# A gated-slot-attention kernel with a Strassen-like product: E's transposes ahead of the 64 by 64 products, and sums, silu pieces and weight pieces in other places

## The chip, the core and the metric

The kernel runs on one core of a Trainium2 chip. The core has TensorE (PE, whose weight loads are shown apart as PEld), VectorE (DVE), ScalarE (ACT), GpSimd (POOL) and SyncE (SP), which here issues all DMAs. The time is device microseconds of one execution. Smaller is better. A profile of one execution gives start and length of every instruction and what released an engine that waited.

## The reference, cut to what matters

Two layers on x of 2 batches by 2048 tokens by 512, all in float32: gated slot attention with 16 heads, and a feed-forward part with a Hadamard transform. Each is added to its input and followed by a layer norm.

```python
q, k, v, s = (to_heads(x @ W) for W in (Wq, Wk, Wv, Ws))     # 64, 64, 128, 64 wide a head
s = clip(s, -32, 32); z = cumlogsumexp(s, time)
g = exp(z[t-1] - z[t]); p = exp(s - z)
hk[t] = hk[t-1] * g + outer(k, p);   ok = q * 64**-0.5 @ hk   # slots of the keys
pv = softmax(ok)
hv[t] = hv[t-1] * g + outer(p, v);   o = pv @ hv
o = o * rsqrt(mean(o**2) + 1e-5) * g_norm_weight
x = layernorm(x + (o * silu(x @ Wg)) @ Wo)
h = fwht(silu(x @ W1.T) * (x @ W3.T))                        # 2048 wide
x = layernorm(x + h @ W2.T)
```

## The kernel before

**Products.** Every large product is done as two by two blocks with seven products in place of eight. Each product needs sums of blocks of both factors, which are made ahead, and its results are added up in PSUM and SBUF afterwards. `LEFT` and `RIGHT` say which of a factor's seven slices product m takes. The order of the seven differs from place to place. For a weight, `Weights` loads three of its blocks into slices 0 to 2 and the fourth into a tile `low`, of which there is one for all weights, and `sums(0)` to `sums(3)` make slices 3, 5, 4 and 6: sum 0 and sum 1 read `low`, sum 2 reads sum 0, sum 3 reads sum 2. Slice 6 is taken by product 3, slice 3 by 5, slice 4 by 6, slice 5 by 7.

**Attention.** The 16 heads go in four groups of four, and each group walks over 16 chunks of 128 tokens, both batches at once: 64 steps. `run(new, now, before, old)` writes out one round by hand and works on four steps at a time: `new` gets its x, `now` makes q, k, s (the products `main("q", k)`, L521) and v, g (`main("v", k)`, L547) and its own slots, `before` makes its values and begins its output product `o` (L764, with `o(1)`, `o(5)`, `o(2)`), and `old` finishes it (`o(3)`, `o(6)`, `o(7)`, `o(4)`; the sums of o into the rows are L760). The order on PE, DVE, ACT and POOL is the order of the text; only SP's queue is ordered by a scheduler. Between the q and the v products stands a block of small products:

- `exp_s`: DVE clips s (L529), ACT takes the exponential twice (e2 in L533, e in L535; a group's first step takes one), POOL adds what was carried (L534).
- `k_transposed` (L567, ACT copies to kr in L569), then `o(4)`.
- `scores` (L598), `scores2` (L673), `share_of_keys` (L608), `share_of_values` (L685): 64 by 64 arrays of PE, sixteen products each. DVE masks the scores (L602, L679) and takes in the shares (L620). The scores lie in PSUM banks 2 and 3, the shares of the values in banks 0 and 1.
- `e_transposed`: four 128 by 128 transposes of e into bank 3 (L573), copied by ACT to eT (L575), which `scores2` reads one step later. Then `running_sum` (L580), whose sums ACT copies (L582) and DVE inverts (`reciprocal`, L591).
- `slots` (L626), `values` (L696), `state_slots` (L635), `state_values` (L705): 64 by 64 arrays again.

After the block come the v products 6, 5, 2, 7, 3, 4; `gated` (ACT L722, DVE L724 and L726, POOL L728 to L731) and `softmax` (DVE L643 to L651, ACT L652, DVE L656 and L657, POOL L658, DVE L662) lie beside them. `o_transposed` (L748) is copied by ACT (L445, L446), DVE and POOL (L448 to L451) into ob, and `silu` (L561) gates.

**A group's end.** In a group's last step (`last`) the next q, k, s weights are loaded and summed, and the next v, g weights loaded, to be summed in the first step of the next group (`changes`). One step later (`o_last`) the next Wo rows are loaded, scaled by half the norm's weight (L438) and summed. All of these sums are DVE's, but Wo's scaling and its second and fourth sum, which are POOL's.

**Weight pieces.** The sums of W1, W2 and W3 for the feed-forward part, and in the last group those of the new x (`block`), are generators that do one piece at each call. A round calls them at places 2, 3 and 4 (`work_on`) and at its end; the last four chunks also call them in `more`.

**Feed-forward.** For each of 8 blocks of x and 4 sets of hidden rows (a unit u), `up` makes seven products of seven (L235). DVE adds the results up (L216), twice a sum of two accumulators is taken (L250, for products 6 and 7), `silu` gates the four results (ACT L193) and leaves the products with the other half and the sums for `down` to POOL, in two pieces each two and three slots later. The first unit begins in the last two rounds of attention and runs beside `last_block`, which prepares the last block's x (transposes L315, DVE differences L321).

Of the kernel before, what the change touches and what calls it, by code (L numbers as in the profile page):

```python
# [9 lines left out]
F32 = mybir.dt.float32  # L10
# [5 lines left out]
P = 128  # L16
# [4 lines left out]
DV = 128  # L21
# [17 lines left out]
def gated_slot_attention_ffn_kernel(  # L39
# [34 lines left out]
    nc.gpsimd.memset(mhalf, -0.5)  # L74
    gn = const.tile([P, 1], F32, name="gn")
    nc.sync.dma_start(out=gn, in_=gnw.rearrange("(p o) -> p o", o=1))

    within = const.tile([P, TH], F32, name="within")
    for h in HALVES:
# [102 lines left out]
    def silu(h, at, src):  # L182

        if at == 11:
            h["hid"] = fp.tile([P, 2, 7, 2 * TQ], F32, name="hid")
            h["a21"] = fp.tile([P, 2, 2 * TQ], F32, name="a21", bufs=1)
        a21 = h["a21"]
        hid = h["hid"]
        place = {11: hid[:, :, 0], 21: hid[:, :, 1], 22: hid[:, :, 2], 12: a21}[at]
        o = place.rearrange("p i (j t) -> p i j t", j=2)  # L190
        v = src.rearrange("p (i j) t -> p i j t", j=2)
        gate, lin = v[:, :, :, 0:TQ], v[:, :, :, TQ:]
        nc.scalar.activation(o, gate, AF.Silu)  # L193

        def piece(i):
            nc.gpsimd.tensor_tensor(o[:, i], o[:, i], lin[:, i], ALU.mult)  # L196
            if at == 12:
                nc.gpsimd.tensor_tensor(hid[:, i, 5], hid[:, i, 0], a21[:, i], ALU.subtract)  # L198
            elif at == 22:
                nc.gpsimd.tensor_tensor(hid[:, i, 3], a21[:, i], hid[:, i, 2], ALU.add)  # L200
                nc.gpsimd.tensor_tensor(hid[:, i, 4], hid[:, i, 3], hid[:, i, 0], ALU.subtract)
            elif at == 21:
                nc.gpsimd.tensor_tensor(hid[:, i, 6], hid[:, i, 1], hid[:, i, 4], ALU.subtract)

        for i in range(2):
            after(2 + i, lambda i=i: piece(i))

    def up(u, h):

# [8 lines left out]
        for i, m in enumerate(OUTER):  # L218
            w, left, right = wt.pop(0), LEFT, xb[RIGHT[m]]
            if i < 6 or u + 1 < NU:  # L220
                wt.append(load_w(u + (i + 1) // 7, (i + 1) % 7))
            to, first = {5: ("v", None), 3: ("w", "v"), 1: ("u", None), 2: ("x", "u")}.get(m, ("u", "u"))
            if to == "v" and "v" not in acc:
                open_acc("v", tag="h2")
            if to == "w" and "w" not in acc:
                open_acc("w", pool=fp)
            if i == 3:
                h["w2"] = w2p.tile([P, 2, 7, HD], F32, name="w2t")
                for j in range(2):
                    nc.sync.dma_start(out=h["w2"][:, j], in_=w2s[p + j * NSET])  # L230
            c = sums(pch, 2 * TQ, "")
            for k in INNER:
                s = c[SUM[k]]
                for j in range(2):
                    nc.tensor.matmul(  # L235
                        s[:, j * TQ : (j + 1) * TQ], lhsT=w[:, LEFT[k], j, :], rhs=right[:, RIGHT[k], :],
                        start=(k in (1, 2, 5) and j == 0), stop=True, skip_group_check=True,
                    )
                b = BLOCK[k]
                if k in (1, 5, 6, 4):  # L240
                    if first is None:
                        nc.scalar.copy(t[to][:, b], s)
                    else:
                        add(t[to], s, b, t[first])
                else:
                    add(t[to], s, b)
                if m in (6, 7) and k in ENDS:
                    o = t["w" if m == 6 else "v"][:, b]

                    (nc.gpsimd if u else nc.vector).tensor_tensor(o, o, t["u"][:, b], ALU.add)  # L250
                if k == 4:
                    if p == NSET - 1 and blk + 1 < NBLK:
                        load_x(blk + 1, RIGHT[m])
                    if m in (2, 6, 7, 4):
                        at, src = {2: (11, "x"), 6: (12, "w"), 7: (22, "v"), 4: (21, "u")}[m]
                        silu(h, at, t[src])
                yield
# [36 lines left out]
    def last_block():  # L294
# [17 lines left out]
        for i, (b, k) in enumerate(todo):  # L312
# [5 lines left out]
            if b:  # L318
                for dst, a, c in ((t1, b12, b11), (b12, b22, b12), (t2, b22, t1), (t4, b21, t2)):
                    dst, a, c = (e[:, :, at] for e in (dst, a, c))  # L320
                    nc.vector.tensor_tensor(dst, a, c, ALU.subtract)  # L321
            yield
        yield
        for m, src in enumerate(parts):
# [25 lines left out]
    with ExitStack() as att:  # L350
# [40 lines left out]
        class Weights:  # L391


            def __init__(self, name, parts, raw=None, pool=wp):
                width = sum(p[1] for p in parts)
                self.t = pool.tile([P, 7, 2, width], F32, name=name)
                self.low = c1.tile([P, 2, width], F32, name="low", tag="low")
                self.raw = raw
                at = 0
                for src, n in parts:  # L400
                    for (i, j), dst in (
# [5 lines left out]
                        )  # L407
                    at += n

            def sums(self, k):  # L410
                t, low = self.t, self.low

                second = nc.vector if self.raw is None else nc.gpsimd
                if k == 0:
                    if self.raw is not None:
                        self.raw(t[:, 0:3])
                        self.raw(low)
                    nc.vector.tensor_tensor(t[:, 3], low, t[:, 2], ALU.add)
                elif k == 1:
                    second.tensor_tensor(t[:, 5], t[:, 0], low, ALU.subtract)  # L420
                elif k == 2:
                    nc.vector.tensor_tensor(t[:, 4], t[:, 3], t[:, 0], ALU.subtract)
                else:
                    second.tensor_tensor(t[:, 6], t[:, 1], t[:, 4], ALU.subtract)

        def rows_of(src, g, width):
            return lambda j: src[j * HD : (j + 1) * HD, g * width : (g + 1) * width]
# [5 lines left out]
            return Weights("wvg", [(rows_of(a, g, HG * DV), HD) for a in (wv, wg)])  # L433

        def load_o(g):
            def scaled(a):

                nc.gpsimd.tensor_scalar(a, a, gn, 0.5, ALU.mult, ALU.mult)  # L438

            at = g * HG * DV  # L440
            return Weights("wo_", [(lambda j: wo[at + 2 * j * DV : at + (2 * j + 2) * DV, :], HD)], scaled, wpo)

        def right_factor(dst, tp):

# [36 lines left out]
        class Step:  # L481
# [88 lines left out]

            def e_transposed(self):
                for i in range(NQ):
                    nc.tensor.transpose(bank(3)[:, i, :], self.e[:, i, :], ident)  # L573
                self.eT = c2.tile([P, NQ, P], F32, name="eT")
                nc.scalar.copy(self.eT, bank(3))  # L575

            def running_sum(self):
                p = pch.tile([P, 512], F32, name="running", tag="c1", bufs=2).rearrange("p (i t) -> p i t", t=P)
# [454 lines left out]
        def run(new, now, before, old):  # L1033
# [12 lines left out]
                        next(ups)  # L1046

            def work_on(place):
                y["place"] = place
                next(pieces[0], None)  # L1050

            def more():

                if old is not None and old.g == NG - 1 and old.n >= NCB - 4:
                    work_on(1)


            g = now.g if now is not None else NG
            last = now is not None and now.final and g + 1 < NG
            o_last = old is not None and old.final and old.g + 1 < NG  # L1060
            opens = now is not None and now.first
            o_opens = o_last or now is steps[0]

            changes = opens and now is not steps[0]

            late = [nw["vg"].sums] if now is steps[0] else []
            if opens:
                w["qks"] = nw.pop("qks")
            main("q", 1)
            do(old, "o", 3)  # L1070
            if new is not steps[1]:
                do(new, "load_x")
            main("q", 2)
# [1 line left out]
            y["second"] = new is not None and new.g > 0  # L1075
            work_on(2)
            if changes:
                nw["vg"].sums(0)
            main("q", 5)
            work_on(3)  # L1080
            if changes:
                nw["vg"].sums(1)
            main("q", 6)
            do(old, "o", 6)
            do(before, "r_transposed")
            if changes:
                nw["vg"].sums(2)
            main("q", 7)
            work_on(4)
            if changes:  # L1090
                nw["vg"].sums(3)
            main("q", 3)
            main("q", 4)
            do(old, "o", 7)
# [16 lines left out]
            do(old, "row_stats", 0)  # L1111
            if o_last:
                nw["o"] = load_o(old.g + 1)

# [3 lines left out]
            do(before, "within2")  # L1120
            do(now, "share_of_keys")
            do(before, "share_of_values")
            do(now, "e_transposed")
            do(now, "running_sum")
            do(old, "normalize")
            do(old, "store_rows")
# [11 lines left out]
            for f in late:  # L1138
                f(1)
            main("v", 5)  # L1140
            do(now, "reciprocal", 1)
            main("v", 2)
            more()
            for f in late:
                f(3)
            if last:
                nw["qks"].sums(0)
            main("v", 7)
            do(now, "softmax")
            main("v", 3)  # L1150
            more()
            if o_opens:
                nw["o"].sums(0)
            do(now, "softmax_sum")
            if o_opens:
                nw["o"].sums(1)
            do(before, "o_transposed")
            if o_opens:
                nw["o"].sums(2)
                nw["o"].sums(3)  # L1160
            do(now, "softmax_end")
            main("v", 4)
            if last:
                nw["vg"] = load_vg(g + 1)
                nw["qks"].sums(1)
            do(now, "tanh")
            if before is not None and before.first:
                w["o"] = nw.pop("o")
            do(before, "o", 1)
            if last:  # L1170
                nw["qks"].sums(2)
            do(before, "o", 5)
            more()
            do(now, "silu")
            do(before, "o", 2)
            if last:
                nw["qks"].sums(3)
            next(pieces[0], None)

            if old is not None and old.g == NG - 1 and NCB - 4 <= old.n < NCB - 2:  # L1180
                rows_transposed_last(old)
# [109 lines left out]
```

## Time and profile before

| | |
|---|---|
| median of 3 executions | 3583.42 us (3582.95 to 3586.16) |
| the profiled execution | 3586.86 us |
| its span, first to last instruction | 3584.7 us |
| mean granted PE clock | 0.996 |
| DMA, mean share of 16 engines | 35.2% |
| a plain step of attention | 36.9 to 38.0 us |
| first product of the first unit beside the rounds | about 2470 us |

The profile is read from the page's shares by engine, then by the waits (who waited for whom, with total, count and longest), then in order of time. A line of that last view has start, length, engine, line, operation, output <- input, form and count of merged instructions, and in brackets how long the engine was idle before and what released it. In order of time the instructions of one step's small products are seen to start 1026.67 (L567), 1028.07 (L598), 1029.51 (L685), 1030.64 (L573), 1031.13 (L580), 1032.09 (L626), 1035.03 (L547).

### The profile page before, as it was taken

What the parts mean: (1) busy time and instruction counts of PE and PEld (TensorE: products, weight loads), DVE (VectorE), ACT (ScalarE), POOL (GpSimd) and SP (SyncE); (2) the same over time, 40 slices, a digit from 0 to 9 for tenths busy, and PEclk for the clock granted to TensorE, in tenths of its full rate; (3) what the DMA queues carried; (4) which work ended last, traced back from release to release, by engine and by line L of the source; (5) the groups of instructions that cost most, each with busy time, mean ns of one, the idle gap of its engine ahead of it and who ended that gap; (6) DMA issues with size and microseconds to landing.
All of it is one profiled execution on the core that took longest, in us unless ns stands there. A gap on an engine that the chain in (4) does not pass through costs nothing. (4 is left out here: it accounts for less than half of the span.)

```text
span 3584.7 us, 76033 instructions
## 1 busy us (share of the span) xinstructions
PE 3505.6 (98%) x32160; PEld 2749.4 (77%) x32160; DVE 2379.1 (66%) x3968; ACT 985.3 (27%) x1768; POOL 1108.0 (31%) x1048
## 2 busy tenths in 40 slices
PE   8999999999999999999999999998899999999998
PEld 6777777777777767777767777766788888888887
DVE  5677677756567756567666677777666766756756
ACT  3333333233333233333333333332111111111110
POOL 2222222212112222212213222223353553553544
PEclk9999999999999999999999999999999999999999
DMA  4433434421112321112221233346636535435432
GB/s 156 123 108 111 140 113 130 128 67 53 63 60 67 116 72 54 65 60 67 83 88 61 66 116 119 131 139 232 210 131 237 182 126 208 161 130 198 167 128 75
DMA packets 229188, 425.08 MB, mean 119 GB/s; under 512 B 20592, under 2 KB 141808, under 8 KB 228848
## 3 DMA queue, kind: packets, MB, share of 16 engines
q1 hardware_dynamic: 228848, 420.22, 35.2%
q8 instruction: 253, 4.15, 0.5%
q14 instruction: 87, 0.71, 0.1%
HBM read 297.47 MB, written 125.30 MB: 118 GB/s over the span
## 5 line engine op out<-in xcount | busy, mean ns | idle before, releaser
L547 PE MATMUL c<-wvg,xb 128*128 128x512 f32 x1792 | 808.0, 596 | 4.5 <-DVE t L479 2.3
L547 PEld LDWEIGHTS c<-wvg,xb 128*128 128x128 f32 x1792 | 321.8, 189 | 365.9 <-issue 289.1
L521 PE MATMUL c<-xb,wqks 128*128 128x128 f32 x3584 | 559.3, 279 | 6.7 <-DVE rows L760 5.0
L521 PEld LDWEIGHTS c<-xb,wqks 128*128 128x128 f32 x3584 | 485.2, 194 | 35.2 <-DVE rows L760 20.0
L216 DVE TENSOR_TENSOR accux<-c,accux 128x512 f32<-128x512 f32 x496 | 340.9, 690 | 180.0 <-PE c L235 163.7
L274 PE MATMUL dc<-w2t,hid 128*128 128x256 f32 x1792 | 455.3, 379 | 2.1 <-DVE res L281 2.1
L235 PE MATMUL c<-wvg,xb 128*128 128x256 f32 x1792 | 431.9, 380 | 7.1 <-DVE accux L216 7.1
L760 DVE TENSOR_TENSOR rows<-c,rows 128x256 f32<-128x256 f32 x448 | 182.1, 417 | 349.6 <-PE c L764 348.0
L235 PEld LDWEIGHTS c<-wvg,xb 128*128 128x128 f32 x1792 | 338.7, 190 | 57.8 <-DVE accux L216 11.2
L274 PEld LDWEIGHTS dc<-w2t,hid 128*128 128x128 f32 x1792 | 340.2, 190 | 49.5 <-DVE res L281 3.3
L521 PE MATMUL c<-wqks,xb 128*128 128x128 f32 x1792 | 350.5, 278 | 2.0 <-DMA wqks<-in_L_attn_Ws 2.0
L479 DVE TENSOR_TENSOR t<-c,kept 128x384 f32<-128x384 f32 (+1 forms) x384 | 229.8, 610 | 168.9 <-PE c L521 164.0
L235 PE MATMUL c<-wqks,xb 128*128 128x256 f32 x1344 | 326.5, 381 | 8.4 <-DVE accv L216 3.0
L474 ACT COPY kept<-c 128x384 f32<-128x384 f32 (+1 forms) x384 | 203.1, 529 | 418.5 <-PE c L521 335.6
L235 PEld LDWEIGHTS c<-wqks,xb 128*128 128x128 f32 x1344 | 255.0, 191 | 47.5 <-DVE accux L216 5.0
L521 PEld LDWEIGHTS c<-wqks,xb 128*128 128x128 f32 x1792 | 275.8, 194 | 2.3 <-DMA wqks<-in_L_attn_Ws 2.3
L281 DVE TENSOR_TENSOR res<-dc,res 128x256 f32<-128x256 f32 x448 | 189.0, 422 | 117.6 <-PE dc L274 106.9
L591 DVE RECIPROCAL iz<-z 128x256 f32<-128x256 f32 x128 | 223.8, 1748 | 45.7 <-ACT z L582 45.7
L728 POOL TENSOR_SCALAR ss<-ss 128x8 f32<-128x8 f32 x64 | 12.6, 197 | 770.7 <-DVE ss L726 770.7
L534 POOL TENSOR_TENSOR e<-e,zc 1x512 f32<-1x512 f32 x60 | 76.4, 1274 | 541.1 <-ACT e L533 539.4
L724 DVE TENSOR_TENSOR t<-po,t 64x512 f32<-64x512 f32 (+1 forms) x192 | 132.3, 689 | 120.3 <-ACT sq L722 119.4
L250 POOL TENSOR_TENSOR accw<-accw,accux 128x512 f32<-128x512 f32 x60 | 75.9, 1275 | 283.1 <-DVE accux L216 281.7
(194 smaller groups left out, 5084.8 us busy)
## 6 DMA issues: line engine op xcount, KB each, us to landing
xb<-w13s SPq DMA_DIRECT2D x112, 896.0 KB
xb<-xd SPq DMA_DIRECT2D x48, 896.0 KB
yd<-rows SPq DMA_DIRECT2D x128, 256.0 KB
w2t<-w2s SPq DMA_DIRECT2D x32, 896.0 KB
rows<-yd SPq DMA_DIRECT2D x100, 256.0 KB
xd<-xb SPq DMA_DIRECT2D x16, 896.0 KB
wvg<-fxd SPq DMA_DIRECT2D x16, 896.0 KB
raw<-in_L_ffn_W SPq DMA_DIRECT2D x48, 256.0 KB
```

The lines of the kernel that those rows point to most:

```text
L216: nc.vector.tensor_tensor(into[:, b], s, (into if first is None else first)[:, b], ALU.add)
L235: nc.tensor.matmul(s[:, j * TQ : (j + 1) * TQ], lhsT=w[:, LEFT[k], j, :], rhs=right[:, RIGHT[k], :], start=(k in (1, 2, 5) and j == 0), st ...
L274: nc.tensor.matmul(s, lhsT=h["hid"][:, i, LEFT[m], k * P : (k + 1) * P], rhs=h["w2"][:, i, RIGHT[m], :], start=(m in (1, 2, 5) and i == 0) ...
L281: nc.vector.tensor_tensor(r, s, r, ALU.add)
L474: nc.scalar.copy(self.kept[k], s)
L479: nc.vector.tensor_tensor(t[:, to], s, self.kept[other], ALU.add)
L521: nc.tensor.matmul(out[:, i * P : (i + 1) * P], lhsT=a, rhs=b, start=(k in OPENS and c == 0 and i == 0), stop=(c == 1), skip_group_check=True,
L534: nc.gpsimd.tensor_tensor(self.e2[0:1], self.e2[0:1], zc, ALU.add)
L547: nc.tensor.matmul(out, lhsT=self.xb[:, RIGHT[k], c, :], rhs=w["vg"].t[:, LEFT[k], c, :], start=(k in OPENS and c == 0), stop=(c == 1), sk ...
L591: nc.vector.reciprocal(self.iz[:, h], self.z[:, h])
L724: nc.vector.tensor_tensor(self.gj[to, j], self.po[j][at], self.gj[to, j], ALU.mult)
L760: nc.vector.tensor_tensor(y_, self.uo.sum(k), y_, ALU.add)
```

## The change

- `e_transposed` stands behind `o(4)`, ahead of the scores, and writes bank 1 instead of bank 3.
- The next group's q, k, s sums: 0, 1 and 3 on POOL, 2 on DVE, the first two ahead of v's product 7, the others behind `o(5)`. The v, g sums: 1 and 3 on POOL.
- Wo's scaling is ACT's (`scale_o`), behind v's product 5; its sums 0, 1 and 3 are POOL's, the first two ahead of v's product 7, the others ahead of `o_transposed`. In the first step all of it stands at the round's end, the sums on DVE.
- Weight pieces are called at places 1 to 4, where 1 stands behind `o(3)`, and not at a round's end. In a group's first round they aren't called.
- In the first unit the sum for product 6 is POOL's, and `last_block`'s differences are. In every unit the first silu's pieces run five slots later.

```diff
+    half_gn = const.tile([P, 1], F32, name="half_gn")
+    nc.gpsimd.tensor_scalar(half_gn, gn, 0.5, 0.0, ALU.mult, ALU.add)
...
-            after(2 + i, lambda i=i: piece(i))
+            after(2 + i + (5 if at == 11 else 0), lambda i=i: piece(i))
...
-                    (nc.gpsimd if u else nc.vector).tensor_tensor(o, o, t["u"][:, b], ALU.add)
+                    (nc.gpsimd if u or m == 6 else nc.vector).tensor_tensor(o, o, t["u"][:, b], ALU.add)
...
-                    nc.vector.tensor_tensor(dst, a, c, ALU.subtract)
+                    nc.gpsimd.tensor_tensor(dst, a, c, ALU.subtract)
...
-            def sums(self, k):
+            def sums(self, k, eng=nc.vector):
...
-                    nc.tensor.transpose(bank(3)[:, i, :], self.e[:, i, :], ident)
+                    nc.tensor.transpose(bank(1)[:, i, :], self.e[:, i, :], ident)
...
-                nc.scalar.copy(self.eT, bank(3))
+                nc.scalar.copy(self.eT, bank(1))
...
             def work_on(place):
-                y["place"] = place
-                next(pieces[0], None)
+                if not changes:
+                    y["place"] = place
+                    next(pieces[0], None)
+
+            def scale_o():
+                for t in (nw["o"].t[:, 0:3], nw["o"].low):
+                    nc.scalar.activation(t, t, AF.Copy, scale=half_gn)
...
             do(old, "o", 3)
+            work_on(1)
...
             if changes:
-                nw["vg"].sums(1)
+                nw["vg"].sums(1, nc.gpsimd)
...
             if changes:
-                nw["vg"].sums(3)
+                nw["vg"].sums(3, nc.gpsimd)
...
             if o_last:
                 nw["o"] = load_o(old.g + 1)
+            do(now, "e_transposed")
...
             do(before, "share_of_values")
-            do(now, "e_transposed")
             do(now, "running_sum")
...
             main("v", 5)
+            if o_last:
+                scale_o()
             do(now, "reciprocal", 1)
             main("v", 2)
...
             if last:
-                nw["qks"].sums(0)
+                nw["qks"].sums(0, nc.gpsimd)
+                nw["qks"].sums(1, nc.gpsimd)
+            if o_last:
+                nw["o"].sums(0, nc.gpsimd)
+                nw["o"].sums(1, nc.gpsimd)
             main("v", 7)
             do(now, "softmax")
             main("v", 3)
             more()
-            if o_opens:
-                nw["o"].sums(0)
             do(now, "softmax_sum")
-            if o_opens:
-                nw["o"].sums(1)
+            if o_last:
+                nw["o"].sums(2)
+                nw["o"].sums(3, nc.gpsimd)
             do(before, "o_transposed")
-            if o_opens:
-                nw["o"].sums(2)
-                nw["o"].sums(3)
             do(now, "softmax_end")
             main("v", 4)
             if last:
                 nw["vg"] = load_vg(g + 1)
-                nw["qks"].sums(1)
             do(now, "tanh")
...
             do(before, "o", 1)
+            do(before, "o", 5)
+            more()
             if last:
                 nw["qks"].sums(2)
-            do(before, "o", 5)
-            more()
+                nw["qks"].sums(3, nc.gpsimd)
             do(now, "silu")
             do(before, "o", 2)
-            if last:
-                nw["qks"].sums(3)
-            next(pieces[0], None)
+            if now is steps[0]:
+                scale_o()
+                for k in range(4):
+                    nw["o"].sums(k)
```

More of the change, by code (lines that the diff above doesn't have):

```diff
@@ L391, in gated_slot_attention_ffn_kernel, with __init__ @@
         class Weights:
-            def __init__(self, name, parts, raw=None, pool=wp):
+            def __init__(self, name, parts, pool=wp):
                 width = sum(p[1] for p in parts)
@@ L397, in __init__ @@
                 self.low = c1.tile([P, 2, width], F32, name="low", tag="low")
-                self.raw = raw
                 at = 0
@@ L408, in __init__ @@
                     at += n
-            def sums(self, k):
+            def sums(self, k, eng=nc.vector):
                 t, low = self.t, self.low
-                second = nc.vector if self.raw is None else nc.gpsimd
                 if k == 0:
[L415 to L418, printed above, removed]
+                    eng.tensor_tensor(t[:, 3], low, t[:, 2], ALU.add)
                 elif k == 1:
-                    second.tensor_tensor(t[:, 5], t[:, 0], low, ALU.subtract)
+                    eng.tensor_tensor(t[:, 5], t[:, 0], low, ALU.subtract)
                 elif k == 2:
-                    nc.vector.tensor_tensor(t[:, 4], t[:, 3], t[:, 0], ALU.subtract)
+                    eng.tensor_tensor(t[:, 4], t[:, 3], t[:, 0], ALU.subtract)
                 else:
-                    second.tensor_tensor(t[:, 6], t[:, 1], t[:, 4], ALU.subtract)
+                    eng.tensor_tensor(t[:, 6], t[:, 1], t[:, 4], ALU.subtract)
         def rows_of(src, g, width):
@@ L435, in load_o @@
         def load_o(g):
-            def scaled(a):
-                nc.gpsimd.tensor_scalar(a, a, gn, 0.5, ALU.mult, ALU.mult)
             at = g * HG * DV
-            return Weights("wo_", [(lambda j: wo[at + 2 * j * DV : at + (2 * j + 2) * DV, :], HD)], scaled, wpo)
+            return Weights("wo_", [(lambda j: wo[at + 2 * j * DV : at + (2 * j + 2) * DV, :], HD)], wpo)
         def right_factor(dst, tp):
@@ L1055, in more @@
                     work_on(1)
+            changes = now is not None and now.first and now is not steps[0]
             g = now.g if now is not None else NG
@@ L1061, in run @@
             opens = now is not None and now.first
-            o_opens = o_last or now is steps[0]
-            changes = opens and now is not steps[0]
             late = [nw["vg"].sums] if now is steps[0] else []
@@ L1077, in run @@
             if changes:
-                nw["vg"].sums(0)
+                nw["vg"].sums(0, nc.vector)
             main("q", 5)
@@ L1086, in run @@
             if changes:
-                nw["vg"].sums(2)
+                nw["vg"].sums(2, nc.vector)
             main("q", 7)
```

## The prediction

> **What bounds the kernel now.** I read the page's busy shares, then the busy time of the stretches between one step's first scores and the next, then TensorE's (PE's) waits, then the instructions in order of time where those point.
>
> ```profile
> PE 3505.6 (98%) x32160; PEld 2749.4 (77%) x32160; DVE 2379.1 (66%) x3968; ACT 985.3 (27%) x1768; POOL 1108.0 (31%) x1048
> ```
>
> PE is the bound and the number of its products stays, so only its pauses can be won. The stretches (us, then busy time of PE, weight loads, VectorE (DVE), ScalarE (ACT), GpSimd (POOL), granted clock, DMA):
>
> ```profile
> 599.40:643.12 43.72, 38.79 (x429) 28.35 (x429) 35.39 (x54) 12.77 (x24) 6.75 (x6) 1.00 0.56 172
> 679.96:724.66 44.70, 40.24 (x406) 30.12 (x405) 30.05 (x48) 12.61 (x25) 14.83 (x11) 0.92 0.35 107
> 1139.51:1176.37 36.86, 36.79 (x421) 27.30 (x421) 26.57 (x39) 12.15 (x24) 8.02 (x7) 1.00 0.17 55
> 1213.40:1255.95 42.55, 37.92 (x422) 27.48 (x421) 33.67 (x50) 11.76 (x23) 10.94 (x14) 1.00 0.48 151
> 1294.07:1339.90 45.83, 40.22 (x412) 29.84 (x411) 24.50 (x36) 13.78 (x27) 14.65 (x11) 0.96 0.24 76
> 1825.72:1868.36 42.64, 39.02 (x422) 28.96 (x421) 31.40 (x42) 11.76 (x23) 6.75 (x6) 0.96 0.38 122
> 1905.01:1947.86 42.85, 38.71 (x406) 28.73 (x405) 25.36 (x38) 11.68 (x23) 14.65 (x13) 0.96 0.19 60
> ```
>
> Row three is a plain step. Against it, and less 0.9 and 1.3 us for weight pieces' products in rows one and five, the steps in which a head group ends (rows 1, 4, 6) lose 6.0, 5.7 and 5.8 us, those that take in the new Wo (2, 5, 7) 7.8, 7.7 and 6.0: 39 us. Of it 8.8 is half clock: (1 - clock) by length gives 3.6, 1.8, 1.7, 1.7. The other place is the feed-forward part's first unit, 2505 to 2550.
>
> ```profile
> PE c L764 <- POOL wo__6775 L424: 3.6, 1, 3.6
> PEld ps L573 <- DVE a L679: 18.8, 62, 1.2
> ...
> 1026.67 0.63 ACT L535 ACTIVATE e<-e 128x512 f32<-128x512 f32 x1
> 1027.11 1.03 PE L764 MATMUL c<-wo__6775,ob 128*128 128x256 f32 x4
> 1030.63 0.42 PEld L573 LDWEIGHTS ps<-ident,e 128*128 128x128 f32 x4 [0.31 <-DVE a L679]
> 1035.03 0.30 PEld L547 LDWEIGHTS c<-wvg,xb 128*128 128x128 f32 x2 [0.17 <-issue]
> ...
> 2021.91 1.03 PE L764 MATMUL c<-wo__17915,ob 128*128 128x256 f32 x4
> 2022.40 0.63 ACT L535 ACTIVATE e<-e 128x512 f32<-128x512 f32 x1
> ...
> 696.00 1.54 POOL L438 TENSOR_SCALAR wo__6775<-wo__6775,gn 128x1536 f32<-128x1536 f32 x1
> 696.66 1.42 DVE L651 TENSOR_TENSOR r<-r,mx 128x512 f32<-128x512 f32 x1
> ...
> 2429.43 0.71 PE L521 MATMUL c<-xb,wqks 128*128 128x128 f32 x4 [1.86 <-DVE rows L760]
> 2509.34 2.67 POOL L196 TENSOR_TENSOR hid<-hid,accux 128x512 f32<-128x512 f32 x2
> 2509.40 2.88 DVE L95 TENSOR_SCALAR rows<-rows,mv,lrs 128x512 f32<-128x512 f32 x2 [0.95 <-POOL lrs L91]
> ```
>
> The reader is to see three things. A return from 64 by 64 arrays to the full one idles the weight loads 0.17 us without a wait, 0.31 with L679's. The exponentials e (L535) are ready at 1027.30, 0.7 before PE could start behind L764 (four starts 0.22 apart: 1027.97); in the last group at 2023.03, 0.25 after 2022.78. And a DVE operation from SBUF to SBUF beside one of POOL waits for it: L651 takes 0.69 alone, here it ends 0.54 after L438 ends, and two L95 (0.54 each) end behind L196. Results that DVE reads from PSUM (L760, L216) aren't lengthened beside POOL.
>
> **A, E's transposes.** Start to start a plain step has 0.31 from L764 to the scores, 0.34 from L685 to L573, 0.49 to L580, 0.96 to L626: 2.10. After: 0.22 to L573, 0.33, 0.20 to the scores (as behind L567 at 58.15), 0.20 from L685 to L580 (as from L705 to L547), 0.32 + 0.43 + 0.31: 2.01. So -0.09 in 48 steps, -4.5: the wait's 0.14 goes, but L580 restarts slower than a transpose. Behind it: `share_of_values` waits for eT's copy (bank 1), done about 0.8 before; L602, L679, L620 end 0.43 later, the last at 1032.46, when L591 can't start before 1032.7. In 13 steps of the last group PE waits for e, 0.25 and 0.11 for signal and restart, less the 0.18 wait for kr that this hides: +2.4. Step 63 sheds 0.8 of a 1.15 wait for L679. Sum -2.9 (from -8, no wait or restart left, to +3).
>
> **B, the group's sums.** L658, a POOL sum of 128x512, takes 1.28; by length a q/k/s sum (768) 1.9, a v/g sum (1024) 2.6. On DVE they take 0.94 and 1.22.
> - Group's end, 17.5 in three. DVE's sum before v7 (L418, 2.08) goes to POOL, which is free from 614.98. L651, ready at 615.7, must let it end at 616.9: +1.05 (0 to 1.9). After o5 DVE keeps one sum of 0.94 ahead of L561 and o2's L760, which q2 awaits: +1.35 (0.95 to 3.1, where POOL's last sum gets in before L561; L651's row says that the earlier runs first, and L561 is, so 1.35). The waits of 1.8 and 1.2 us for o3 and q5 go, since sums and weight pieces no longer stand there. On SP's queue all v/g pieces now stand behind `low`, which waits for POOL's sum until 619.3 (issued at 623.96 in the profile); 2 MB at some 300 GB/s land by 628. The first v/g sum waits for them on DVE, o6's L760 and q7's L479 behind it, q4 behind those: +0.5 (0 to 1.6). Left 2.9 each: -8.8.
> - New Wo, 21.5 in three. The scaling (POOL 1.54 and 1.12) becomes two ACT operations of 1.5 and 0.6 (from `th`, 1.06 for 1024), on an ACT idle from 691.6 to 698.1; its DMAs were issued by 681.7, and L652 stands behind: 0 (to +1). Two sums on POOL stand before L658; L651 waits +0.4. DVE's sum stands before L448: o5 +0.7 (0.3 to 1.2). POOL's last stands before L450, and L662 lets it pass: o3 and q2 +1.2 (0.4 to 3). L424's wait and the half clock go. Left 2.3 each, and 2.0 at 1299.7 that no engine caused: -12.6.
> - The first group's sums come later, as many: 0 (-1 to +1.5). `half_gn`, one POOL instruction of 0.2 while POOL has nothing until 8.2: 0.
>
> Sum -21.4.
>
> **C, weight pieces.** The call at a step's end moves behind the next o3; none run in a group's first step. At 2427 four DVE pieces stand before o3's L760: the 1.86 and the half clock behind it (2430 to 2434, 1.7) go: -3.6. In 14 steps a piece's product fills the 0.23 that PE waits before q2: -3.2 (to 0). Else DVE is idle where they land (1.65 before L760 at 1025.15). Sum -6.8.
>
> **D, first unit.** L196 five slots later frees L95: 1.9 of the 2.96 us that PE waits at 2510. Four L250 (0.69) and eight L321 (0.42) leave DVE; PE waits 0.7, 1.7 and 1.1 beside them. POOL needs 3 us for each four L321, then 5.1 for L250, and the next sums wait for that: 1.0 back. Sum -4.4 (-8 to 0).
>
> The profiled execution took 3586.86 (span 3584.7), 3.4 above the median of 3583.42; differences against its span are applied to the median: 3583.4 - 35.5 = 3548.
>
> **Rules against the rows.** The three waits over 3 us in rows two, five and seven each have half clock behind them, those of 1.8, 0.5 and 1.2 in a row one time in three; I leave none over 1.4 and take none. The Trainium skill, page TensorE: Matmul & The Clock Gate, section "Part 1: The HAM clock gate", gives one idle window of about 3.4 us as the trigger; by it the last group's end would not have halved, and the row shows it did, so a remainder stays possible (rival 1). Its page GPSIMD Engine Reference, section "3.1 Elementwise", measures a `tensor_tensor` add at 1.96 times VectorE's time and says to keep such work on VectorE. An estimate by that, 5 us longer in each of three groups if POOL were what is waited for, would make the sum 3563. The rows have POOL busy 8 of 37 us, and I follow them.
>
> **Rivals.**
> 1. POOL's sums hold DVE up and the clock still halves: 0.85 + 1.75 more in three group ends (7.8), 1.7 in four steps (6.8), D nothing (4.4): 3567. For it L651's row; against it POOL's idle time before its sums.
> 2. DVE slips in between: lower ends of B (-5.9 and -4.8) and D (-3.6): 3534. For it: PSUM reads don't wait.
> 3. It cancels: A at +3, a quarter of B, C and D nothing: 3581. Against it: L424's wait alone is 3.6 and surely goes.
> 4. Slower: weight pieces between q7 and `exp_s` make e late in every step, at L573 before the scores. To pass 3590.6 it must outweigh the other parts' 32.6 by 7.2, 0.83 in each of 48 steps, so e 1.5 us later than now. At 1.7 it gives 3599. Before L529 DVE has 0.71 and 1.65 idle, and the longest piece is two sums of 1.0.
>
> **Numbers.** Forecast 0.57 (own range 3538 to 3558), rivals 0.20, 0.10, 0.06, 0.07. The range 3533 to 3571 leaves out rivals 3 and 4 and some of 1 and 2. The measurement tells 0.2% (7.2 us): faster 0.87, same 0.06, slower 0.07.
>
> **What would show it.** L573 behind L764 without L679's wait, and waiting for e in the last group only; the six late steps at 39 to 40 us with the clock mostly at 1.00; POOL sums of 1.9 with L651 over 1 us; no L521 wait at 2427; no L250 `accw` on DVE. I am wrong if q2's waits at a group's end exceed 2 us, or if L535 releases PE in plain steps.

## The result, and the profile after

The changed kernel takes 3613.72 us (median of 4 runs, 3608.76 to 3617.14) beside 3584.79 us of the kernel before (4 runs, 3582.95 to 3587.48). The ratio is 1.0078, 95% interval 1.0064 to 1.0092: slower by 28 us (23 to 33). The forecast was 3548 us, faster. The profiled execution of the changed kernel took 3608.76 us (span 3607.0), 22 us over that of before.

Lines of the changed kernel stand some six lower from L430 on (E's transposes were L573 and are L567, kr's copy L569 and L563, the sums of o L760 and L754, q's sums L479 and L473) and three or four higher before that (L196 is L199, L95 is L98, L235 is L239). The page's busy shares:

```profile
PE 3513.8 (97%) x32160; PEld 2747.3 (76%) x32160; DVE 2354.6 (65%) x3940; ACT 994.7 (28%) x1776; POOL 1142.8 (32%) x1069
```

PE has as many products, so the time is in its pauses again. The stretches from step to step (us, then busy time of PE, weight loads, DVE, ACT, POOL, granted clock, DMA):

```profile
606.94:646.18 39.24, 37.47 (x422) 27.45 (x421) 26.41 (x37) 11.57 (x22) 18.15 (x11) 1.00 0.42 134
683.94:724.36 40.42, 37.83 (x405) 27.44 (x404) 26.50 (x45) 14.76 (x26) 13.79 (x10) 1.00 0.39 119
1142.27:1179.30 37.03, 36.85 (x421) 27.25 (x420) 26.75 (x39) 12.17 (x23) 8.02 (x7) 1.00 0.18 57
1217.08:1256.84 39.76, 37.64 (x421) 27.48 (x420) 26.42 (x37) 11.57 (x22) 18.14 (x11) 1.00 0.43 138
1294.02:1334.41 40.39, 38.02 (x410) 27.62 (x409) 24.35 (x39) 15.35 (x27) 15.53 (x14) 1.00 0.35 100
1828.17:1866.82 38.65, 37.06 (x422) 27.35 (x421) 26.18 (x37) 11.58 (x22) 18.14 (x11) 1.00 0.40 130
1903.70:1943.49 39.79, 37.67 (x405) 27.38 (x404) 24.71 (x39) 14.76 (x26) 14.80 (x13) 1.00 0.20 63
2140.38:2178.98 38.60, 37.50 (x429) 28.18 (x428) 28.71 (x51) 13.20 (x24) 9.60 (x12) 1.00 0.31 103
2217.58:2260.19 42.61, 37.76 (x429) 28.25 (x428) 27.94 (x50) 13.19 (x24) 10.16 (x13) 1.00 0.47 162
```

The six late steps (all but rows three, eight and nine) went from 262.3 us to 238.3 and have the full clock. So B's gain is there, 24 us. It is lost elsewhere: the median of the plain steps (the 41 outside the groups' ends) rose from 38.03 to 38.33 us (row three is the one shown of before, 36.86 there), and the last group's steps, 37.5 us each before, take 38.6 (row eight), five of them 40.1 to 42.6 (row nine). PE's and its weight loads' waits name the releaser:

```profile
PEld ps L567 <- ACT kr L563: 53.8, 64, 3.1
PE ps L567 <- ACT kr L563: 28.4, 58, 2.7
PE c L515 <- DVE t L473: 5.2, 4, 2.7
```

E's transposes (L567) wait for ACT's copy of **k's** transposes, in 64 of 64 steps. In order of time, a plain step, a step of the last group, a block piece in the last group, and the first unit:

```profile
1102.99 0.63 ACT L529 ACTIVATE e<-e 128x512 f32<-128x512 f32 x1
1103.43 1.03 PE L758 MATMUL c<-wo__6763,ob 128*128 128x256 f32 x4
1103.53 0.57 ACT L468 COPY kept<-c 128x512 f32<-128x512 f32 x1
1104.00 0.59 ACT L563 COPY kr<-ps 128x512 f32<-128x512 f32 x1
1104.64 0.66 PE L567 MATMUL ps<-ident,e 128*128 128x128 f32 x4 [0.18 <-ACT kr L563]
...
2138.15 0.63 ACT L529 ACTIVATE e<-e 128x512 f32<-128x512 f32 x1
2139.15 0.59 ACT L563 COPY kr<-ps 128x512 f32<-128x512 f32 x1
2139.80 0.44 PE L567 MATMUL ps<-ident,e 128*128 128x128 f32 x2 [1.10 <-ACT kr L563]
...
2249.59 0.42 DVE L795 TENSOR_TENSOR halves<-yq 128x256 f32<-128x256 f32 x1 [5.93 <-DMA yq<-yb]
2251.06 0.42 DVE L754 TENSOR_TENSOR rows<-c,rows 128x256 f32<-128x256 f32 x1
2251.39 0.55 DVE L473 TENSOR_TENSOR t<-c,kept 128x384 f32<-128x384 f32 x1
2251.99 0.71 PE L515 MATMUL c<-xb,wqks 128*128 128x128 f32 x4 [2.73 <-DVE t L473]
...
2527.56 2.67 POOL L199 TENSOR_TENSOR hid<-hid,accux 128x512 f32<-128x512 f32 x2
2527.62 2.88 DVE L98 TENSOR_SCALAR rows<-rows,mv,lrs 128x512 f32<-128x512 f32 x2 [0.95 <-POOL lrs L94]
2531.76 1.13 PE L239 MATMUL c<-wqks,xb 128*128 128x256 f32 x4 [2.96 <-DVE accv L220]
```

In the plain step e is ready at 1103.62 and PE's last start of L758 is 1104.08, but L567 starts at 1104.64, 0.05 after kr's end at 1104.59. In the last group it starts 0.06 after kr's end and 1.0 after e's. Four DVE differences of the block (L795 to L798) stand before L473 and wait 5.93 us for their load, and PE waits 2.73 for L473. And L98 still runs beside POOL's L199, with the same 2.88 and 2.96 us as before.

Three theories come out of this. **1:** the move of E's transposes costs 30 to 40 us, because banks 0 and 1 are halves of one tile (`ps[0]`), and the wait that is set for a write to the tile counts the readers of the other bank too. **2:** the weight pieces' new places cost what they win, because the block's first piece now stands a place earlier, ahead of its load. **3:** the five slots of silu's pieces move nothing. The rival to 1 is that e itself is late (rival 4 of the prediction) by the pieces' work on DVE.

### The profile page after: what moved, and what is told of

It is laid out like the page before. It is cut to its first block, busy times and chain, and to the rows that moved or that the text cites. A ratio compares the mean times of both kernels' runs of the same rounds, so it can differ in the third digit from the quotient of the medians.

```text
span 3607.0 us, 76143 instructions
## 1 busy us (share of the span) xinstructions
PE 3513.8 (97%) x32160; PEld 2747.3 (76%) x32160; DVE 2354.6 (65%) x3940; ACT 994.7 (28%) x1776; POOL 1142.8 (32%) x1069
## 5 line engine op out<-in xcount | busy, mean ns | idle before, releaser
L239 PE MATMUL c<-wvg,xb 128*128 128x256 f32 x1792 | 434.9, 382 | 7.1 <-DVE accux L220 4.6
L754 DVE TENSOR_TENSOR rows<-c,rows 128x256 f32<-128x256 f32 x448 | 181.5, 417 | 340.4 <-PE c L758 335.5
L239 PEld LDWEIGHTS c<-wvg,xb 128*128 128x128 f32 x1792 | 341.0, 191 | 58.9 <-DVE accux L220 8.1
L239 PE MATMUL c<-wqks,xb 128*128 128x256 f32 x1344 | 325.1, 380 | 6.6 <-DVE accv L220 3.0
L473 DVE TENSOR_TENSOR t<-c,kept 128x384 f32<-128x384 f32 (+1 forms) x384 | 229.2, 609 | 147.6 <-PE c L515 141.9
L239 PEld LDWEIGHTS c<-wqks,xb 128*128 128x128 f32 x1344 | 253.8, 190 | 45.6 <-DVE accux L220 5.3
```

The lines of the kernel that those rows point to most:

```text
L239: nc.tensor.matmul(s[:, j * TQ : (j + 1) * TQ], lhsT=w[:, LEFT[k], j, :], rhs=right[:, RIGHT[k], :], start=(k in (1, 2, 5) and j == 0), st ...
L473: nc.vector.tensor_tensor(t[:, to], s, self.kept[other], ALU.add)
L754: nc.vector.tensor_tensor(y_, self.uo.sum(k), y_, ALU.add)
```

## The experiments

### Without E's move, and E's move alone

```diff
 # no_e_move: the changed kernel, but
-            do(now, "e_transposed")        # behind o(4), bank(1)
...
             do(before, "share_of_values")
+            do(now, "e_transposed")        # bank(3)
```

> The changed kernel with e_transposed back behind share_of_values and back in bank 3; all else of the change stays. Theory 1 (E's transposes in bank 1 wait for ACT's copy kr, because banks 0 and 1 are one tile, 0.34 us in a plain step and 1.26 in one of the last group): the products' pauses around the block add up to 34 us in the changed kernel's trace, so 3613.7 - 34 = 3580 us, 3575 to 3586. Rival (the move is as forecast, the loss is DVE work of the weight pieces that makes e late): 3613.7 + 3 = 3617 us, and the wait before the scores or L567 stays.

> The kernel before with nothing but e_transposed ahead of the scores and in bank 1. Theory 1: 48 plain steps by +0.30, 13 of the last group by +0.9 to 1.1, 3584.8 + 27 = 3612 us, up to 3618 where the clock halves in the last group. Rival (weight pieces make e late): their places are those of before, so my forecast of -2.9 for the move stands, 3582 us.

Measured: without the move 3564.35 us, ratio 0.9933 (0.9918 to 0.9948) to the kernel before; the move alone 3630.16 us, 1.0116 (1.0099 to 1.0133), +42 us (36 to 48). Theory 1 stands, the rival falls: the pieces' places are those of before in the second kernel, and L573 waits for kr in 64 of 64 steps all the same. Both came out beyond the numbers expected (3575 to 3586 and 3612 to 3618). The span of the move alone is 44 us longer than that of the kernel before: 33 of it lie in the block's transitions, 3 are more half clock, and 7 lie in pauses that are taken up under the findings on the hardware.

### The two banks as two tiles

```diff
-        ps = [pps.tile([P, 2, 512], F32, name=f"ps{i}") for i in range(2)]
+        ps = [pps.tile([P, 512], F32, name="ps0a"), pps.tile([P, 2, 512], F32, name="ps1")]
+        ps0b = pps.tile([P, 512], F32, name="ps0b")
...
+            if at < 2:
+                return (ps[0], ps0b)[at].rearrange("p (i t) -> p i t", t=width)
```

> The changed kernel with banks 0 and 1 as two tiles of one bank each, so that E's transposes wait for no reader of bank 0; copies of both banks become two. Theory 1: in plain steps e is ready before PE is, 48 times 0.34 us go; in the last group 1.26 becomes 0.36 (e itself), 13 times 0.9; with 2 to 3 us of half clock 3584 us (3580 to 3590). Rival (PE waits for e or restarts late in any case): 3612 to 3616 us, with L567's waits as they are.

Measured: 3569.96 us (3567.78 to 3574.78), ratio 0.9951 (0.9936 to 0.9965), 44 us under the changed kernel's 3613.72. That is 10 us below the range expected: between the two traces 33 of 38 us lie in the block's transitions, and the rest is not accounted for. No wait of E's transposes for kr is left. In order of time, the same two places of this kernel (L532 is e, L566 kr, L570 E's transposes):

```profile
1092.49 0.63 ACT L532 ACTIVATE e<-e 128x512 f32<-128x512 f32 x1
1092.93 1.03 PE L761 MATMUL c<-wo__6764,ob 128*128 128x256 f32 x4
1093.49 0.59 ACT L566 COPY kr<-ps0a 128x512 f32<-128x512 f32 x1
1093.79 0.60 PE L570 MATMUL ps0b<-ident,e 128*128 128x128 f32 x4
...
2113.46 0.63 ACT L532 ACTIVATE e<-e 128x512 f32<-128x512 f32 x1
2114.15 0.66 PE L570 MATMUL ps0b<-ident,e 128*128 128x128 f32 x4
2114.47 0.59 ACT L566 COPY kr<-ps0a 128x512 f32<-128x512 f32 x1
```

The same transposes into the same bank now start 0.29 before kr's copy ends, right behind L761, and in the last group 0.06 after e. So in plain steps the changed kernel waited neither for the bank nor for e, but for the tile. With this the four transitions that the prediction costed are measured as it had them:

| start to start, sum of the four | before | forecast | changed | banks split |
|---|---|---|---|---|
| plain step (median of 41) | 2.10 | 2.01 | 2.40 | 2.01 |
| last group (median of 12) | 2.00 | 2.36 | 3.32 | 2.36 |

### kr's copy ahead of another copy

```diff
-            main("v", 1)
+            if now is not None:
+                now.v(1, False)            # the product without its copy to kept
+            else:
+                main("v", 1)
...
             do(now, "k_transposed")
...
+            if now is not None:
+                now.uv.into(now.t2, 1)
```

> The changed kernel with ACT's copy of v's first product (kept) behind the copy kr in place of ahead of it: kr ends some 0.5 us earlier, e is untouched. Theory 1: nearly all of 0.34 goes in plain steps and 0.4 of 1.26 in the last group's, 48 x 0.3 + 13 x 0.4 = 20, 3594 us (3590 to 3600). Rival (e is what is late): no change, 3612 to 3616 us.

Measured: 3585.61 us (3578.01 to 3591.41), ratio 0.999 (0.998 to 1.000), 28 us under the changed kernel (the range expected was 3590 to 3600; in the traces the block's transitions give 25 of 27 us). E is untouched, and PE's waits for kr fall from 28.4 us to:

```profile
PE ps L568 <- ACT kr L564: 11.9, 16, 1.9
```

The median start from L758 to E's transposes is 0.22 in plain steps (0.56 in the changed kernel) and 0.99 in the last group (1.48). This confirms theory 1 a second time, with the tile as it was.

### The sums alone

> The kernel before with the group's sums, their places and Wo's scaling as in the changed kernel, and nothing else of the change. By the prediction's B: -21.4 us. From the trace without E's move: the nine late steps lose 24 to 26 us less, so a ratio of 0.993 to 0.994 (24 of 3590). Rival (POOL's sums hold DVE up and the clock halves, rival 1): -7 us, 0.998, with half clock at the group's ends.

The edit is the change's own diff of `Weights.sums`, `load_o`, `scale_o` and their calls. Measured: 3568.19 us beside 3587.11, ratio 0.9958 (0.9944 to 0.9971), -15 us (-20 to -10), less than either number expected. The stretches of the six late steps:

```profile
599.11:640.52 41.41, 38.18 (x429) 28.24 (x429) 32.38 (x49) 12.77 (x24) 18.32 (x11) 1.00 0.56 172
677.36:717.05 39.69, 37.73 (x406) 27.43 (x405) 27.37 (x47) 14.69 (x27) 13.76 (x10) 1.00 0.41 120
1205.60:1246.61 41.01, 37.35 (x422) 27.37 (x421) 31.35 (x45) 11.75 (x23) 22.62 (x19) 1.00 0.50 157
1284.32:1325.60 41.28, 38.54 (x412) 27.99 (x411) 23.15 (x35) 15.75 (x29) 13.77 (x10) 1.00 0.26 84
1812.44:1851.58 39.14, 37.33 (x422) 27.48 (x421) 26.48 (x37) 11.75 (x23) 18.15 (x11) 1.00 0.41 133
1888.23:1927.32 39.09, 37.46 (x405) 27.35 (x404) 23.83 (x37) 13.76 (x25) 13.76 (x12) 1.00 0.21 65
```

They add up to 241.6 us beside 262.3: -20.7 in the profiled pair, all at the full clock. POOL's sums beside DVE don't make a new bound.

### The weight pieces alone, and the first unit alone

> The kernel before with nothing but the weight pieces' calls as in the changed kernel (places 1 to 4, none at a round's end, none in a group's first round). By the prediction's C: -6.8 us, 0.998. Theory 2 (the block's first piece now stands a place earlier, behind q5, and DVE waits there for its load, before o3's sum and q's copies): -3.6 for 2427, +5 for PE's waits in steps 53, 57 and 61, +1.7 to 3.4 of half clock behind them, group steps as before: +1 to +5 us, 1.000 to 1.0015.

> The kernel before with nothing but the first unit's changes (silu's first pieces five slots later, the sums for product 6 and last_block's differences on POOL). By the prediction's D: -4.4 us. Theory 3 (the five slots move nothing, since POOL has no instruction in them and L196 follows its last L91 either way: the 2.96 us before L235 stays): -1.9 less of it, -1 to -4 us, 0.999 to 1.000, with L95 of 2.88 and PE's wait of 2.96 in the trace.

The edits are the change's own diffs of `work_on` and its calls, and of `after`, L250 and L321. Measured: the pieces 3591.77 us, ratio 1.0009 (1.0000 to 1.0017), +3 us (0 to 6); the unit 3584.88 us, ratio 0.9993 (0.9984 to 1.0001), -3 us (-6 to 0). With the pieces alone twelve of the last group's steps take 459.7 us in place of 450.7. The pause at 2427 (1.86, with half clock behind it) is replaced by one of 1.17 a product earlier, without half clock: DVE's L561 now stands there beside work of POOL's, and takes 1.75 us in place of 1.21.

```profile
2430.28 1.75 DVE L561 SCALAR_TENSOR_TENSOR t<-th,t 128x1024 f32<-128x1024 f32 x1
2432.42 0.71 PE L521 MATMUL c<-xb,wqks 128*128 128x128 f32 x4 [1.17 <-DVE rows L760]
```

With the unit alone PE's pause behind L95 is as long as before. The four parts alone add up to 42 - 15 + 3 - 3 = +27 us; the change as a whole measured +28. That they agree is in part luck: without the move the change measured -24 (-29 to -19), where the other three parts add up to -15, so the move cost some 10 us more inside the change than alone. The intervals just allow both.

### The block's first piece a place later

```diff
             b11, b12, b22, b21 = load(0, 0), load(0, 1), load(1, 1), load(1, 0)
             yield
             yield
+            yield
             inner(0, b11)
```

> The changed kernel with E's transposes in their old place, and one more yield in block() ahead of its first inner, so that this piece stands at place 4 as in the kernel before. Theory 2: PE's waits for q's copies in steps 53, 57 and 61 go, 5 us and 3.4 of half clock in the trace without E's move: 3564.4 - 8 = 3556 us. Rival (the last group is longer because PE takes in other work): no change, 3564 us.

> The same kernel as no_e_later, as the base of the three runs beside it on the same chip: 3555 us, 3551 to 3560.

Measured: 3555.27 us, ratio 0.9912 (0.9899 to 0.9926), and in a second set 3554.60 us, 0.9909 (0.9893 to 0.9926). Without the added yield it was 0.9933, so some 8 us come from one `yield` (the two intervals overlap; in the traces the same twelve steps of the last group take 450.6 us in place of 461.2). The last group's steps are back at 37.5 us; here are the two that rows eight and nine show of the changed kernel:

```profile
2107.66:2145.16 37.50, 37.49 (x429) 28.25 (x428) 28.70 (x51) 13.18 (x25) 9.60 (x12) 1.00 0.31 106
2182.67:2220.18 37.51, 37.50 (x429) 28.25 (x428) 26.67 (x46) 13.19 (x25) 9.60 (x12) 1.00 0.48 162
```

### What else could be won

```diff
 # e_early_in_three: no_e_later with banks 0 and 1 as two tiles, and
             if o_last:
                 nw["o"] = load_o(old.g + 1)
+            do(now, "e_transposed", 1)     # returns unless g < NG - 1
...
-            do(now, "e_transposed")
+            do(now, "e_transposed", 3)     # returns unless g == NG - 1
```

> no_e_later with E's transposes ahead of the scores in the first three groups only, banks 0 and 1 as two tiles, and in the last group in their old place. By the transitions measured with the split bank (0.22, 0.20, 0.20 in place of 0.31, 0.34, 0.11): -0.09 us in each of 48 steps, -4.3 us against no_e_later. Rival (what goes in one place comes back in another, such as later copies): no difference.

```diff
-            after(2 + i + (5 if at == 11 else 0), lambda i=i: piece(i))
+            after(2 + i + (15 if first and at == 11 else 0), lambda i=i: piece(i))
```

(`first` is true in the first unit.)

> no_e_later with the first silu's pieces of the first unit 15 slots later in place of 5, which puts them behind last_block's first four differences in POOL's order. Theory 3 (only a place behind other POOL instructions takes them from under L95): two L95 of 0.54 to 0.6 in place of 2.88, PE's wait of 2.96 down to 1.1, -1.9 us, and up to 3 us of half clock less behind it. Rival (the next product's weights land no earlier): PE's wait for them grows by the 1.9 and nothing is won.

> e_early_in_three and silu_pieces_15 together, the fastest version that the theories can give: 3555 - 4.3 - 1.9 = 3549 us (3545 to 3555).

Measured beside no_e_later_again's 3554.60 us: e_early_in_three 3557.14 (0.9919, 0.9905 to 0.9934), silu_pieces_15 3552.91 (0.9908, 0.9893 to 0.9923), both 3554.81 (0.9913, 0.9898 to 0.9928). None is faster beyond the noise, and the four executions of the first (3557.06 to 3559.01) all lie above the four of the base (3552.71 to 3554.92). In the first, plain steps have a median of 37.94 in place of 38.03 us, the 0.09 of the forecast, but their sum is 1548.4 beside 1548.2: pauses within the 64 by 64 products that no engine caused take it back (8.3 us of them beside 4.9). The first unit of silu_pieces_15, in order of time:

```profile
2475.32 1.00 DVE L98 TENSOR_SCALAR rows<-rows,mv,lrs 128x512 f32<-128x512 f32 x2 [0.95 <-POOL lrs L94]
2477.58 1.13 PE L239 MATMUL c<-wqks,xb 128*128 128x256 f32 x4 [1.08 <-DVE accv L220]
...
2488.08 1.73 PE L239 MATMUL c<-wvg,xb 128*128 128x256 f32 x4 [2.26 <-DMA xb<-w13s]
2488.62 2.49 POOL L199 TENSOR_TENSOR hid<-hid,accux 128x512 f32<-128x512 f32 x2
```

and of no_e_later_again:

```profile
2477.28 2.67 POOL L199 TENSOR_TENSOR hid<-hid,accux 128x512 f32<-128x512 f32 x2
2481.49 1.13 PE L239 MATMUL c<-wqks,xb 128*128 128x256 f32 x4 [2.96 <-DVE accv L220]
...
2490.75 1.10 PE L239 MATMUL c<-wvg,xb 128*128 128x256 f32 x4 [1.02 <-DMA xb<-w13s]
```

Fifteen slots put L199 behind POOL's first four L325; L98 runs alone (1.00 for two), and PE's wait falls by 1.88. Of that 1.24 come back at the next product, whose weights (xb) land no earlier. So the rival was two thirds right.

Of the versions that beat both kernels, no_e_later is the simplest of the fastest: the change without E's move and with one more yield, 0.9% under the kernel before.

## Why the prediction was wrong, point by point

**A, E's transposes: the step that failed.** It was -2.9 us and is +42 (36 to 48) by itself. The step asked when e is ready and which later writers wait for eT's copy in bank 1. It didn't ask what the first write to bank 1 has to wait for: kr's copy, which reads bank 0 of the same tile. The upper bound of +3 went with it. The profile before had the row that was needed; ACT's copies and the block's piece of the kernel before, in order of time:

```profile
1138.12 0.63 ACT L535 ACTIVATE e<-e 128x512 f32<-128x512 f32 x1
1139.12 0.59 ACT L569 COPY kr<-ps 128x512 f32<-128x512 f32 x1
...
2243.44 0.42 DVE L801 TENSOR_TENSOR halves<-yq 128x256 f32<-128x256 f32 x1 [1.37 <-DMA yq<-yb]
```

kr ends at 1139.71, after e by 0.96, while L764's last start was 1139.20 and E's transposes were to start at 1139.42. The 0.34 of each plain step could have been read off, had the wait been known. The same sum with it gives +0.30 in a plain step and +1.32 in one of the last group (table above), less the wait for kr at L608 that goes there (0.18): 48 x 0.30 + 13 x 1.14 = 29 us. The transitions of 62 steps are 33 us longer in the trace of the move alone and 35 in that of the changed kernel; half clock and the pauses named below come on top. The costs of the transitions themselves were right to 0.01 us.

The trigger wasn't e, so rival 4 had the place and the sign (PE at L573 waits before the scores in every step) but the wrong cause, weight pieces ahead of L529, and the wrong size: 1.0 us in each of 48 steps, where 0.34 was measured, and 1.26 in the last group's. Its 3599 us lie nearer to the result by luck. Its chance of 0.07 was too low, because e was the only input that was looked at. Neither of the two signs of being wrong came, q2's waits over 2 us or a release by L535 in plain steps: they watched e as well, and the release came from kr.

On the Trainium skill, page Perfetto Trace Analysis, section "Matmuls": it says that independent groups of matmuls should rotate through different PSUM banks, so that ACT's or DVE's reading of one overlaps the next group's products. Here ACT's copy of k's transposes and the transposes of e were in different banks and did not overlap (0.56 from L758 to L567), and did when the banks were two tiles (0.22). The measurement narrows the rule: in this kernel the waits go by tile.

**B, the group's sums: right in the stretches, some 6 us short in the runs.** Forecast -21.4, measured -20.7 in the six stretches and -15 (-20 to -10) in the runs, without half clock in any of the six. With the sums alone L645 (L651 before) beside POOL's sum takes 1.55 us in the first group's end, by 0.86 more than alone; forecast was 1.05 more. q2 waits 1.57 there, against 1.35; in the changed kernel it is 1.42 and 0.89. POOL's sums take 1.82, 2.27 and 2.73 (estimated 1.9) and 2.35 (2.6). Rival 1's half clock didn't come, nor the estimate of 5 us for each group by the 1.96 of the Trainium skill (GPSIMD Engine Reference, section "3.1 Elementwise"): the sum of 768 was 1.9 to 2.9 times as long on POOL as DVE's 0.94, but no wait of PE's names a POOL sum.

**C, weight pieces: the second step that failed.** Forecast -6.8, measured +3 (0 to 6). At 2427 some 2.4 of the 3.6 came: the half clock went, but 0.69 of a pause's 1.86 is all that PE won there. Of -3.2 for filled waits before q2, 1.5 came (the sum of the 40 plain steps after the first). What was left out: "Else DVE is idle where they land" was taken from a plain step of the second group. In the last group the pieces are the block's, and the first of each waits for a load. Before the change it stood at place 4 and waited 1.37 with q3's sum behind it (last row above). At place 3 it stands ahead of o6's and q's next sums. PE waited 2.73, 0.19 and 1.92 for them in three steps of the changed kernel; with the pieces alone 2.26 and 2.41, and 1.3 each in two steps for kr, which then came late. Without E's move half clock followed two of these waits (2.21 and 2.50).

**D, first unit: near, by another way.** Forecast -4.4, measured -3 (-6 to 0). The 1.9 from L95 did not come: slots count places in the text, and POOL, in order, has no instruction of its own between the old place and the new one; L196 follows the last L91 in both. The rest, DVE without L250 and L321, shows in the trace: PE's waits of 1.73 and 1.12 there became 0.35 and 0.46, while the next grew from 1.82 to 2.11. In the runs the interval reaches 0.

**The total.** -35.5 was forecast. The parts measured alone: +42, -15, +3, -3. Without the failed step of A the forecast was -32.6, and the change without E's move measured -24.

## What to carry to other kernels

Before a write is moved ahead, list every reader and writer of the whole tile that it writes into, the other bank's too, and put each one's end beside the new start; two banks in one tile were one buffer to the waits here. A piece of work that begins with a load is placed by the landing of the load in the stage where it runs, not by where DVE was idle in another stage. And a place in one engine's queue changes only if an instruction of the same engine is passed: read the order on that engine before a shift is costed.

## What the runs showed of the hardware that was not expected

**Pauses within the 64 by 64 products.** Every trace has 4 to 19 pauses of 0.15 to 2.6 us before these short products which the profile puts to no engine ("issue"), such as this one of e_early_in_three:

```profile
1811.29 0.92 PE L695 MATMUL po<-t,a 64*64 64x128 f32 x25 [1.43 <-issue]
```

They come to 3.9 us in the kernel before, 9.8 in the changed one, 11.1 with E's move alone, 12.2 in kr_first, 8.6 in split_bank and 8.3 in e_early_in_three; without the move to 3.9 to 7.1. One kernel with E early (both_places) has 5.1. The traces of the changed kernel and of no_e_move differ by 44 us in span, 35 in the block's transitions and 6 in these pauses; so a part of what E's move cost beyond the count lies here. The traces tell one thing of the long ones. Of the 26 that last 1.2 us or more, 24 have a transfer of DMA queue q8, which the page of the profile lists as "instruction", under way in them or ended less than 0.1 us before; of the 101 shorter ones none has. Of stretches of that length taken at random a quarter have one. The loading of instructions is therefore a suspect for the long pauses, but no run was made to test it, and what makes the short ones, and more of them with E early, is open.

**Half clock after less than 3.4 us.** In the changed kernel PE idled 2.69 us before 2099.68, and from about 2100.2 the granted clock was 0.5 for 3.4 us; 2.12 us before 2259.61 (with 2.73 us ten us earlier) did the same, 2.09 before 2418.77 (with 1.92 seven us earlier) did not. The Trainium skill, page TensorE: Matmul & The Clock Gate, section "Part 1: The HAM clock gate", gives an idle window of about 3.4 us that runs free; the length of the halved stretches agrees, but an idle time well under it was enough here. In the kernel before, 1.86 us before 2429.43 were enough once: the clock was 0.5 from 2430.5. In the six late steps of the changed kernel, where no wait is longer than 1.63 us, no stretch was halved.
